# Layer 0's norm by node tile along the free axis, with the first chunk of neighbour sums in its loop, and layer 1's reciprocal denominators through memory

## The chip, the cores and the metric

The kernel runs on one core of one Trainium2 chip. The metric is the device time of one execution in microseconds; the time of a kernel is the median of its runs.

## The reference

Four graph layers stand one after the other, each on the normed and rectified input and each with a residual. The batch is 8, there are 2048 nodes with 64 features, and 64 hyperedges.

```python
h = jnp.maximum(_layernorm(x, axis=-1), 0.0)
x = x + L0(h, H, adj, ...)   # layer 0
h = jnp.maximum(_layernorm(x, axis=-1), 0.0)
x = x + L1(h, adj, W, a)     # layer 1
...                          # layers 2 and 3 in the same form
```

Layer 0 has two halves whose results are mixed by a learned softmax. One is the mean over neighbours, `einsum('nm,bmf->bnf', adj / deg, h @ W_ind)`, called `industry` below. The other goes through the hyperedges of each node. Layer 1 is a masked attention over the neighbours:

```python
e = leaky_relu(s_src[:, :, None] + s_dst[:, None, :], 0.2)
attention = softmax(where(adj > 0.5, e, -9e15), axis=2)
return elu(attention @ h)
```

Layers 2 and 3 are repeated products with the adjacency matrix, small maps of the features, and in layer 3 a map that differs from node to node.

## The kernel before

The 8 batches make 4 pairs, `NP`; a pair's 2 x 64 features fill 128 partitions. The 2048 nodes make 16 tiles of 128 (`NT`) and 4 chunks of 512 (`NCW`). A tensor named with T, or `hn[p]`, has features on the partitions and nodes along the free axis.

The program is written with a tile framework. Its scheduler puts the instructions into each engine's queue in an order of its own, and can move loads, memsets and products forward. Where an order is to hold, the code says so: `InOrder` keeps each instruction of an engine in written order, and `kit.strict` does this for matrix products and transposes. Each queue runs in its order, so an instruction that waits holds up all behind it. The SP queue issues most loads and stores, and the POOL queue (GpSimd) issues the adjacency loads and the DMAs that add into memory.

Layer 0, as far as it matters here:

- **Norm** (L882 to L912): for each pair and each half of the nodes (`HN` = 1024), `x` is loaded from `xT` with features on the partitions. `kit.norm` (L739) gets mean and variance by products with `kit.avg`, a 128x128 matrix that averages over each batch's 64 partitions, then Square, Ln and Exp on ScalarE and the rest on VectorE. The result `hn[p]` is multiplied with `W_ind` (`py`, L902) and stored as two parts `Y[0]`, `Y[1]`, high and low.
- Between the pairs come `pairs` (L833, numbers the pairs of node and hyperedge: `rank`, `Q`, `slot`, `mid`, `width`), `weights` (L813) and the weights of layers 1 and 2.
- **Industry** (L926): for each chunk of 512 nodes, eight loads `at` of two row tiles of the adjacency, and for each row tile 4 pairs x 2 parts = 8 products into the four banks `acc`. VectorE adds the adjacency rows (`ds`, L945) for the degrees. After a row tile's 8 products, one entry of the list `units` is run. `units` holds the other half's work: `members` (L963; products `ph`, `pg`, `pd`; stores to `hi_dram` and `lo_dram`), the tables and the bias rows of layer 3. At a chunk's end the sums are moved to `ev`, divided by the degree (`rdeg`) and stored.

The gather stage of layer 0 follows at about 248 us, then its output stage, and from about 495 us layer 1.

**Layer 1** (`attend`, L1543) runs for each pair and each half of the nodes, so 8 times. For each of the 16 row tiles `m`, VectorE makes two score tiles `pt` (L1572), and TensorE multiplies them into `o` (features) and `dn` (denominators, each repeated over 32 partitions). In the next half's loop, `between(m)` runs the leftovers of the last: at m = 1 `total(0)`, at m = 2 `end`. `total(k)` spreads the denominators to the 64 partitions of each batch with a product by the matrix `wide` (`prd`, L1586) and takes Ln; `end` does the second one, Exp, and `res = o * den` (L1593), the ELU and a DMA that adds into `x1_dram`.

Of the kernel before, what the change touches and what calls it, by code (L numbers as in the profile page):

```python
# [8 lines left out]
FP = mybir.dt.float32  # L9
# [625 lines left out]
class Kit:  # L635


    def __init__(self, tc, t, pool):
# [13 lines left out]
        self.wide = pool.tile([P, P], FP, name="wide")  # L652
        nc.vector.memset(self.wide, 0.0)
        for q in range(4):
            nc.vector.memset(self.wide[32 * q : 32 * q + 32, half(q % 2)], 1.0 / 32)
# [19 lines left out]
    def block_diag(self, pool, src, name):  # L675
        return self.block_diag_in(pool.tile([P, P], FP, name=name), src)
# [7 lines left out]
    def layer1_weights(self, pool, ps):  # L684

        nc, t = self.nc, self.t
        W = self.block_diag(pool, t["L1_gnn_W"], "W1f")
        WT = self.block_diag(pool, t["L1_gnn_WT"], "W1Tf")
        a4 = pool.tile([P, 4], FP, name="a4")
        nc.vector.memset(a4, 0.0)  # L690
        for b2 in range(2):
            nc.sync.dma_start(out=a4[half(b2), b2 : b2 + 1], in_=t["L1_gnn_a"][F : 2 * F, :])
            nc.sync.dma_start(out=a4[half(b2), 2 + b2 : 3 + b2], in_=t["L1_gnn_a"][0:F, :])
        nc.vector.tensor_copy(self.W1x[:, 0:P], W)
        pw = ps.tile([P, 4], FP, tag="yy", name="pw1")
        nc.tensor.matmul(pw, WT, a4, start=True, stop=True)
        nc.vector.tensor_copy(self.W1x[:, P : P + 4], pw)

    def layer2_weights(self, pool, ps):
# [5 lines left out]
        W2n = self.block_diag(pool, t["L2_gnn_W2"], "W2n")  # L705
# [4 lines left out]
        for dst, w in ((self.Wvc, self.W1v), (self.Wec, self.W1e)):  # L710
            pw = ps.tile([P, P], FP, tag="yy", name="pw2")
            mm(pw, W2n, w, start=True, stop=True)
            nc.vector.tensor_copy(dst, pw)
        pw = ps.tile([P, 1], FP, tag="yy", name="pwc")
        mm(pw, self.W1v, self.b2c, start=True, stop=True)
        nc.vector.tensor_add(self.b1c, pw, self.b1)
        r = pool.tile([P, P], FP, name="b2r")
        for h in range(2):
            nc.vector.tensor_scalar(r[:, half(h)], self.ones, self.b2c, None, op0=OP.mult)
        pw = ps.tile([P, P], FP, tag="yy", name="pwb")  # L720
# [41 lines left out]
def layer0(kit, hn, x1_dram, open_early, late_tile, between):  # L762
# [40 lines left out]
    with ExitStack() as sA:  # L803
# [9 lines left out]
        def weights(pool, ps):  # L813

            W = kit.block_diag(pool, t["L0_gnn_W"], "W0f")
            WT = kit.block_diag(pool, t["L0_gnn_WT"], "W0Tf")
# [12 lines left out]
            pw = ps.tile([P, 4], FP, tag="yy", name="pw")  # L829
# [3 lines left out]
        def pairs(pool, ps):  # L833


            tmp = pool.tile([P, SLOTS], mybir.dt.int32, name="iota_i")
            nc.gpsimd.iota(tmp, pattern=[[1, SLOTS]], base=0, channel_multiplier=0)
            nc.vector.tensor_copy(slot, tmp)
            tri = pool.tile([P, P], FP, name="tri")
            nc.gpsimd.iota(tmp[:, 0:P], pattern=[[1, P]], base=0, channel_multiplier=-1)  # L840
            nc.vector.tensor_copy(tri, tmp[:, 0:P])
            nc.vector.tensor_scalar(tri, tri, 0.0, None, op0=OP.is_ge)
            for h in range(2):
                nc.sync.dma_start(out=M[:, :, h, :], in_=t["L0_gnn_H"].rearrange("(t p) e -> p t e", p=P))
            Mf = M.rearrange("p t h e -> p (t h e)")
            nc.vector.tensor_scalar(Mf, Mf, 0.0, None, op0=OP.is_gt)
            nc.sync.dma_start(out=MT, in_=t["HT"])
            nc.vector.tensor_scalar(MT, MT, 0.0, None, op0=OP.is_gt)
            rank = pool.tile([P, NT, E], FP, name="rank")
            deg = pool.tile([P, NT], FP, name="deg")  # L850
            first = pool.tile([P, NT], FP, name="first")
            past = pool.tile([P, NT], FP, name="past")
            for g in range(2):
                pr = ps.tile([P, 8, E], FP, tag="yy", name="pr")
                for k in range(8):
                    i = 8 * g + k
                    mm(pr[:, k, :], MT[:, i * P : (i + 1) * P], tri[0:E, 0:E], start=True, stop=True)
                nc.vector.tensor_copy(rank[:, 8 * g : 8 * g + 8, :], pr)
            nc.vector.tensor_copy(deg, rank[:, :, E - 1])
            pc = ps.tile([P, NT], FP, tag="yy", name="pc")  # L860
            mm(pc, tri, deg, start=True, stop=True)
            nc.vector.tensor_copy(past, pc)
            nc.vector.tensor_sub(first, past, deg)

            nc.vector.tensor_tensor(rank, rank, first[:, :, None].to_broadcast([P, NT, E]), op=OP.add)
            nc.vector.tensor_tensor(rank, rank, M[:, :, 0, :], op=OP.mult)
            for h in range(2):
                nc.vector.tensor_scalar(Q[:, :, h, :], rank, -1.0, None, op0=OP.add)
            nc.vector.tensor_tensor(mid, first, past, op=OP.add)
            nc.vector.tensor_scalar(mid, mid, -0.5, 0.5, op0=OP.mult, op1=OP.add)  # L870
            nc.vector.tensor_scalar(width, deg, 0.5, None, op0=OP.mult)

            lo = pool.tile([P, NT], FP, name="bad_t")
            nc.vector.tensor_reduce(bad[:, 0:1], deg, AX.X, OP.min)
            nc.vector.tensor_scalar(bad[:, 0:1], bad[:, 0:1], 0.5, None, op0=OP.is_lt)
            nc.vector.tensor_scalar(lo, past, SLOTS + 0.5, None, op0=OP.is_gt)
            nc.vector.tensor_reduce(bad[:, 1:2], lo, AX.X, OP.max)
            nc.vector.tensor_reduce(bad[0:E, 2:3], MT, AX.X, OP.max)
            nc.vector.tensor_scalar(bad[0:E, 2:3], bad[0:E, 2:3], 0.5, None, op0=OP.is_lt)


        with ExitStack() as s1:  # L882
            pool = s1.enter_context(tc.tile_pool(name="rank", bufs=1, reuse_waits="tile"))
            sb = s1.enter_context(tc.tile_pool(name="nf_sb", bufs=2, reuse_waits="tile"))
            ps = s1.enter_context(tc.tile_pool(name="nf_ps", bufs=2, space=PSUM, reuse_waits="tile"))
            kit.use_ln_exp()
            for p in range(NP):
                for hf in range(2):
                    s = cols(hf, HN)
                    x = sb.tile([P, HN], FP, tag="x", name="x", bufs=3)  # L890
                    for k in range(2):
                        nc.sync.dma_start(out=x[:, cols(k)], in_=t["xT"][p, :, cols(2 * hf + k)])
                    mean = ps.tile([P, HN], FP, tag="mean", name="mean", bufs=1)
                    var = ps.tile([P, HN], FP, tag="var", name="var")
                    xc = sb.tile([P, HN], FP, tag="xc", name="xc")
                    q = sb.tile([P, HN], FP, tag="q", name="q")
                    kit.norm(hn[p][:, s], x, mean, var, xc, q)
                    for c in (2 * hf, 2 * hf + 1):
                        py = ps.tile([P, 4, P], FP, tag="yy", name="py")
                        for k in range(4):  # L900
                            m = 4 * c + k
                            mm(py[:, k, :], hn[p][:, m * P : (m + 1) * P], W_ind, start=True, stop=True)  # L902
                        yh = Y[0][:, 4 * c : 4 * c + 4, p, :]
                        nc.scalar.copy(yh, py)
                        nc.vector.tensor_tensor(Y[1][:, 4 * c : 4 * c + 4, p, :], py, yh.bitcast(FP), op=OP.subtract)
                if p == 0:
                    pairs(pool, ps)
                if p == 1:
                    weights(pool, ps)
                    kit.layer1_weights(pool, ps)  # L910
                if p == 2:
                    kit.layer2_weights(pool, ps)  # L912

        with ExitStack() as s1:
            sp = s1.enter_context(tc.tile_pool(name="streamf", bufs=6, reuse_waits="tile"))
# [10 lines left out]
            def industry(c):  # L926

                acc = [ps.tile([P, CW], FP, tag=f"acc{p}", name=f"acc{p}") for p in range(NP)]
                ds = sb.tile([P, 2, CW], FR, tag="ds", name="ds")
                for g in range(NT // 2):  # L930
                    at = sp.tile([P, 2, CW], FR, tag="at", name="at")
                    nc.gpsimd.dma_start(
                        out=at,
                        in_=t["adjT"][g * 2 * P : (g + 1) * 2 * P, cols(c)].bitcast(FR).rearrange("(k p) n -> p k n", p=P),
                    )
                    for k in range(2):
# [4 lines left out]
                        if units:  # L941
                            units.pop(0)()
# [3 lines left out]
                    was = at  # L946
                ev = [sb.tile([P, CW], FP, tag="ev", name="ev", bufs=4) for p in range(NP)]
# [147 lines left out]
            last = None  # L1095
            for i in range(NT):
                begin_, part_, end_ = members(i)
                units += [begin_, part_] + ([last] if last else [])
                last = end_
            units += [last, table_1]  # L1100
# [4 lines left out]
            for c in range(NCW):  # L1105
# [274 lines left out]
class Layer1:  # L1380
# [6 lines left out]
    def __init__(self, kit, x1_dram):  # L1387
# [5 lines left out]
        self.r_dram = dram.tile([NP, 2, N], FP, name="r_dram")  # L1393
# [702 lines left out]
```

## Time and profile before

| | us |
|---|---|
| runs: median (lowest, highest) of 3 | 2019.26 (2017.56, 2027.6) |
| profiled execution | 2014.73 |
| its span on the core | 2012.8 |
| norm of layer 0, from the start | 70 |
| neighbour sums, four chunks | 70 to 248 |
| gather stage and output stage | 248 to 495 |
| layer 1's attention | 495 to 916 |
| layers 2 and 3 | 916 to the end |

The profile is of one execution. PE is TensorE's products, PEld its weight loads, DVE is VectorE, ACT ScalarE, POOL GpSimd, SP the engine that issues DMAs. A group's line gives line, engine, operation, output<-inputs, tile shape and count, then the busy time, the mean of one in ns, and the engine's idle time just before with what ended it. A timeline's line begins with start and length. A product of float32 operands has two records. Matrix products are pipelined, so a record lasts longer than the time to the next one's start.

### The profile page before, as it was taken

What the parts mean: (1) busy time and instruction counts of PE and PEld (TensorE: products, weight loads), DVE (VectorE), ACT (ScalarE), POOL (GpSimd) and SP (SyncE); (2) the same over time, 40 slices, a digit from 0 to 9 for tenths busy, and PEclk for the clock granted to TensorE, in tenths of its full rate; (3) what the DMA queues carried; (4) which work ended last, traced back from release to release, by engine and by line L of the source; (5) the groups of instructions that cost most, each with busy time, mean ns of one, the idle gap of its engine ahead of it and who ended that gap; (6) DMA issues with size and microseconds to landing.
All of it is one profiled execution on the core that took longest, in us unless ns stands there. A gap on an engine that the chain in (4) does not pass through costs nothing.

```text
span 2012.8 us, 23432 instructions
## 1 busy us (share of the span) xinstructions
PE 1955.4 (97%) x9124; PEld 1153.8 (57%) x9124; DVE 1215.2 (60%) x1899; ACT 444.3 (22%) x827; POOL 294.8 (15%) x399
## 2 busy tenths in 40 slices
PE   7999899978999999999999999999999999999997
PEld 4777777623323223227776467775477755577654
DVE  6666499966888888883234752326632356533366
ACT  4312255566112121112130011210111200112100
POOL 0211077621000000000001210002200012101022
PEclk8999999999999999999999999999999999999999
DMA  6666264176011111114110011201022100122000
GB/s 175 199 182 190 80 225 141 43 216 129 28 43 37 48 37 32 47 28 92 55 45 22 19 43 60 58 12 31 23 63 61 32 22 20 44 62 57 11 19 13
DMA packets 84248, 138.14 MB, mean 69 GB/s; under 512 B 32752, under 2 KB 33008, under 8 KB 81456
## 3 DMA queue, kind: packets, MB, share of 16 engines
q1 hardware_dynamic: 65200, 83.86, 14.3%
q0 software_dynamic: 18928, 52.70, 10.4%
q8 instruction: 74, 1.21, 0.2%
q14 instruction: 46, 0.38, 0.1%
HBM read 102.64 MB, written 37.03 MB: 69 GB/s over the span
## 4 chain that ended last, share of the span: by engine, by line
PE 79%; issue 7%; DVE 4%; DMA 3%; ACT 3%; POOL 2%; SPq 1%; POOLq 0%; ACTq 0%; DVEq 0%
PE acc L726 27%; PE u L726 13%; PE o L726 11%; PE dn L726 6%; PE acc L940 3%; PE pd L726 3%; PE pgs L726 2%; PE py L726 2%; PE var L726 2%; PE mean L726 2%; PE pm L726 1%; DMA iv<-ind_dram 1%; DMA at<-in_adjT 1%; PE ph L726 1%; PE pv L726 1%
## 5 line engine op out<-in xcount | busy, mean ns | idle before, releaser
L726 PE MATMUL acc<-aT,parts 128*128 128x512 f32 x1664 | 448.3, 415 | 0.0
L726 PEld LDWEIGHTS acc<-aT,parts 128*128 128x128 f32 x1664 | 306.4, 188 | 102.3 <-issue 39.8
L1972 DVE TENSOR_TENSOR pr<-u,embf 128x512 f32<-128x512 f32 x256 | 170.6, 688 | 171.4 <-PE u L726 163.7
L1572 DVE SCALAR_TENSOR_TENSOR pt<-R,wd,aT 128x1024 f32<-128x1024 f32 x192 | 236.5, 1280 | 18.2 <-PE dn L726 6.6
L726 PE MATMUL u<-W3f,y 64*128 64x512 f32 x1024 | 244.3, 589 | 0.0
L726 PE MATMUL o<-pt,hS 128*64 128x512 f32 x1024 | 236.4, 599 | 0.8 <-DVE pt L1572 0.6
L726 PEld LDWEIGHTS u<-W3f,y 64*128 64x128 f32 x1024 | 102.9, 187 | 117.9 <-issue 117.9
L726 PEld LDWEIGHTS o<-pt,hS 128*64 128x64 f32 x1024 | 68.0, 136 | 159.2 <-issue 150.5
L726 PE MATMUL u<-W3f,v 64*128 64x512 f32 x512 | 138.9, 607 | 0.0
L940 PE MATMUL acc<-at,Y 128*128 128x512 f32 x512 | 134.1, 406 | 1.8 <-DVE ev L949 1.8
L726 PE MATMUL dn<-pt,vd 128*32 128x512 f32 x1024 | 123.1, 598 | 0.0
L1984 POOL TENSOR_TENSOR fold<-fold 128x256 f32<-128x256 f32 x64 | 47.8, 746 | 506.6 <-DVE fold L1983 506.6
L1789 DVE TENSOR_TENSOR yb<-py,cb_f 128x512 f32<-128x512 f32 x32 | 22.1, 691 | 165.2 <-PE py L726 165.2
L940 PEld LDWEIGHTS acc<-at,Y 128*128 128x128 f32 x512 | 93.5, 191 | 21.8 <-DVE ev L949 2.6
L726 PE MATMUL acc<-aTl,parts 128*128 128x512 f32 x384 | 96.5, 393 | 0.0
L1976 DVE TENSOR_TENSOR pr<-pr 128x512 f32<-128x512 f32 x128 | 88.3, 690 | 2.2
L1572 DVE SCALAR_TENSOR_TENSOR pt<-R,wd,aTl 128x1024 f32<-128x1024 f32 x64 | 79.8, 1282 | 11.4 <-PE dn L726 8.2
L1879 POOL TENSOR_TENSOR bq<-bq,xp 128x512 f32<-128x512 f32 x16 | 20.6, 1290 | 434.1 <-ACT xp L1862 434.1
L726 PEld LDWEIGHTS u<-W3f,v 64*128 64x128 f32 x512 | 51.8, 186 | 56.1 <-issue 34.3
L726 PEld LDWEIGHTS acc<-aTl,parts 128*128 128x128 f32 x384 | 72.1, 188 | 16.9
L726 PEld LDWEIGHTS dn<-pt,vd 128*32 128x32 f32 x1024 | 26.7, 108 | 80.8 <-issue 74.6
L630 POOL TENSOR_TENSOR mix<-ex,wt 128x512 f32<-128x512 f32 x64 | 67.8, 1061 | 34.8 <-DVE ex L630 29.0
(332 smaller groups left out, 2668.5 us busy)
## 6 DMA issues: line engine op xcount, KB each, us to landing
at<-in_adjT POOLq DMA_DIRECT2D x32, 512.0 KB, 4.7
raw<-in_adjT SPq DMA_DIRECT2D x64, 256.0 KB, 3.4
aT<-in_adjT POOLq DMA_DIRECT2D x12, 1024.0 KB, 5.3
xp<-xd SPq DMA_DIRECT2D x45, 256.0 KB, 3.4
R<-r_dram SPq DMA_DIRECT2D x14, 512.0 KB, 3.8
hi_dram<-hi SPq DMA_DIRECT2D x16, 264.0 KB, 2.4
lo_dram<-lo SPq DMA_DIRECT2D x16, 264.0 KB, 3.5
hhi<-hi_dram POOLq DMA_DIRECT2D x16, 264.0 KB, 3.1
```

What stands on the lines that cost most here:

```text
L630: self.tc.keep_in_program_order(getattr(self.engine, name)(*args, **kw))
L726: one = self.nc.tensor.matmul(*args, **kw)
L940: mm(acc[p], Y[h][:, m, p, :], at[:, k, :], start=m + h == 0, stop=m == NT - 1 and h == 1)
L1572: nc.vector.scalar_tensor_tensor(pt, R[b2], wd[:, m, b2 : b2 + 1], aT[m][:, s].bitcast(FP), op0=OP.max, op1=OP.mult)
L1789: nc.vector.tensor_tensor(yb, py, bias[:, None, :].to_broadcast([P, 4, P]), op=OP.add)
L1879: nc.gpsimd.tensor_add(bq, bq, xp)
L1972: nc.vector.tensor_tensor(a, u[h], emb[:, i, 8 * w : 8 * w + 8, None].to_broadcast([P, 8, F]), op=OP.mult)
L1976: nc.vector.tensor_add(pr[h], pr[h], a)
L1984: nc.gpsimd.tensor_add(fold[:, :, 0:2, :], fold[:, :, 0:2, :], fold[:, :, 2:4, :])
```

## The change

The norm of layer 0 is made for each tile of 128 nodes, with the nodes on the partitions, from a new input `xN` (a copy of x in the order node, batch, feature). Sums over 64 features are VectorE reduces along the free axis; GpSimd subtracts the mean, ScalarE squares, VectorE scales. Four transposes for each tile (`turns`) bring it into `hn`'s layout. The products with `W_ind`, the two parts of `Y`, and the 8 products of the first chunk's sums for this tile follow in the same loop with lags of 3, 4 and 5 tiles. The loop has 21 passes; all four engines are kept in written order. In this chunk GpSimd adds the degrees.

The numbering of the pairs becomes `listing`, seven entries for the list of units; the weights of layers 1 and 2 become two more. `weights` and two comparisons (`marks`) stand ahead of the second chunk. The remaining three chunks run two units after the first row tile of a load and one after the second.

In layer 1, ScalarE takes Ln and Exp of the denominators in place; a DMA writes one row for each batch and chunk to memory (`d_dram`), and two DMAs read them back spread over 64 partitions into `den`. `total` and the matrix `wide` go. `end` is run at m = 3.

```diff
+            def load(i):
+                xs[i] = sb.tile([P, B * F], FP, tag="x", name="x", bufs=5)
+                nc.sync.dma_start(out=xs[i], in_=t["xN"][i * P : (i + 1) * P, :])
+            def sums(i):
+                st[i] = sb.tile([P, 2, B], FP, tag="st", name="st", bufs=4)
+                V.tensor_reduce(st[i][:, 0], groups(xs[i]), AX.X, OP.add)
+                V.tensor_scalar(st[i][:, 0], st[i][:, 0], -1.0 / F, None, op0=OP.mult)
+            def centred(i):
+                xc[i] = sb.tile([P, B * F], FP, tag="xc", name="xc", bufs=4)
+                G.tensor_tensor(groups(xc[i]), groups(xs[i]), spans(st[i][:, 0]), op=OP.add)
+            def squares(i):
+                A.activation(xs[i], xc[i], AF.Square)
+            def sums2(i):
+                V.tensor_reduce(st[i][:, 1], groups(xs.pop(i)), AX.X, OP.add)
+            def scales(i):
+                A.activation(st[i][:, 1], st[i][:, 1], AF.Ln, bias=kit.eps, scale=1.0 / F)
+                A.activation(st[i][:, 1], st[i][:, 1], AF.Exp, scale=-0.5)
+            def scaled(i):
+                V.scalar_tensor_tensor(
+                    groups(xc[i]), groups(xc[i]), 0.0, spans(st.pop(i)[:, 1]), op0=OP.max, op1=OP.mult
+                )
+            def turns(i):
+                tp[i] = ps.tile([P, NP, P], FP, tag="tp", name="tpx")
+                x = xc.pop(i)
+                for p in range(NP):
+                    kit.turn(tp[i][:, p, :], x[:, p * P : (p + 1) * P])
+            def turned(i):
+                d = tp.pop(i)
+                for p in range(NP):
+                    A.activation(hn[p][:, i * P : (i + 1) * P], d[:, p, :], AF.Copy)
+            def maps(i):
+                py[i] = ps.tile([P, NP, P], FP, tag="yy", name="py")
+                for p in range(NP):
+                    kit.mm(py[i][:, p, :], hn[p][:, i * P : (i + 1) * P], W_ind, start=True, stop=True)
+            def halves(i):
+                A.activation(Y[0][:, i], py[i], AF.Copy)
+                V.tensor_tensor(Y[1][:, i], py.pop(i), Y[0][:, i].bitcast(FP), op=OP.subtract)
+            def spread(m):
+                for p in range(NP):
+                    for h in range(2):
+                        kit.mm(acc[p], Y[h][:, m, p, :], at[m // 2][:, m % 2, :], start=m + h == 0, stop=m == NT - 1 and h == 1)
+            def degrees(g):
+                if g:
+                    G.tensor_tensor(ds, (at[0] if g == 1 else ds).bitcast(FP), at[g].bitcast(FP), op=OP.add)
...
+            for i in range(4):
+                load(i)
+            for g in range(6):
+                at[g] = rows_of(0, g)
...
+            kit.strict = True
+            for j in range(NT + 5):
+                on = lambda k: 0 <= j - k < NT
+                if 0 < j and j + 3 < NT:
+                    load(j + 3)
+                for lag, step in (
+                    (0, sums), (0, centred), (1, squares), (1, sums2), (2, turns), (3, maps),
+                    (4, halves), (1, scales), (1, scaled), (2, turned), (5, spread),
+                ):
+                    if on(lag):
+                        step(j - lag)
+                m = j - 5
+                if m > 0 and m % 2:
+                    degrees(m // 2)
+                    if 1 <= m // 2 and m // 2 + 5 < NT // 2:
+                        at[m // 2 + 5] = rows_of(0, m // 2 + 5)
+            kit.strict = False
...
-                        if units:
-                            units.pop(0)()
+                        for _ in range(2 - k):
+                            if units:
+                                units.pop(0)()
...
+            weights(small, ps)
+            marks()
+            last, rest = None, listing(ps)
+            rest += [lambda: kit.layer1_weights(small, ps), lambda: kit.layer2_weights(small, ps)]
             for i in range(NT):
                 begin_, part_, end_ = members(i)
                 units += [begin_, part_] + ([last] if last else [])
+                if i % 2 and rest:
+                    units.append(rest.pop(0))
                 last = end_
+            units += rest
...
-            for c in range(NCW):
+            out_of(0, acc, ds)
+            for c in range(1, NCW):
                 industry(c)
...
         nc.vector.tensor_scalar_max(ds, dn, 1e-30)
+        nc.scalar.activation(ds, ds, AF.Ln)
+        nc.scalar.activation(ds, ds, AF.Exp, scale=-1.0)
+        rows = self.d_dram[hf]
+        nc.gpsimd.dma_start(out=rows, in_=ds.rearrange("(q r) n -> q r n", r=32)[:, 0, :])
         den = sb.tile([P, HN], FP, tag="den", name="den", bufs=1)
-        def total(k):
-            pr = ps.tile([P, CW], FP, tag="r", name="prd", bufs=1)
-            mm(pr, wide[half(k), :], ds[half(k), :], start=True, stop=True)
-            nc.scalar.activation(den[:, cols(k)], pr, AF.Ln)
+        for b2 in range(2):
+            nc.gpsimd.dma_start(
+                out=den[half(b2), :].rearrange("p (k n) -> p k n", k=2),
+                in_=rows.rearrange("(k b) n -> b k n", b=2)[b2 : b2 + 1].to_broadcast([F, 2, CW]),
+            )
         def end():
-            total(1)
-            nc.scalar.activation(den, den, AF.Exp, scale=-1.0)
             r = sb.tile([P, HN], FP, tag="res", name="res", bufs=1)
...
-        return [lambda: total(0), end]
+        return [lambda: None, lambda: None, end]
```

## The prediction

> **What bounds the kernel now.** I read the page's engine shares first, then the sliced busy rows, then the busy table over stretches that I cut at the stages, then groups and timelines inside the two stages that the change touches. From the page:
>
> ```profile
> PE 1955.4 (97%) x9124; PEld 1153.8 (57%) x9124; DVE 1215.2 (60%) x1899; ACT 444.3 (22%) x827; POOL 294.8 (15%) x399
> ...
> PE   7999899978999999999999999999999999999997
> ```
>
> TensorE is in use nearly everywhere, and the weak digits stand at the very start and near 200 and 410 to 500 us. A busy PE is modelled and need not run at full rate, so I look at stretches (columns: length; busy us and instructions of PE, weight load, DVE, ACT, POOL; granted clock; DMA share; GB/s):
>
> ```profile
> 0.00:70.00 70.00, 56.86 (x239) 35.27 (x240) 43.82 (x94) 34.81 (x40) 5.96 (x14) 0.93 0.61 172
> 70.00:247.00 177.00, 168.26 (x807) 133.28 (x805) 106.01 (x270) 36.36 (x121) 23.34 (x33) 0.98 0.54 163
> ...
> 500.00:930.00 430.00, 429.30 (x2325) 134.38 (x2325) 367.74 (x372) 74.53 (x124) 6.85 (x8) 1.00 0.16 39
> ```
>
> The first stretch is layer 0's norm. Nothing is full there: PE idles 13 us, and part of its busy time runs at half rate (below). The second is the four chunks of neighbour sums, bound by PE (95%). The third is the attention of layer 1: PE is full, DVE has 62 us to spare. So PE work taken out of the third stretch should pay nearly in full, and PE work of the second that can be laid into the holes of the first pays too.
>
> In the first stretch the norm's means and variances are products with a 128x128 averaging matrix:
>
> ```profile
> L726 PE MATMUL mean<-x,avg_f 128*128 128x512 f32 x32 | 19.3, 728 | 6.7 <-DMA x<-in_xT 4.1 <-DVE xc L745 2.5
> L726 PE MATMUL var<-q,avg_f 128*128 128x512 f32 x32 | 16.4, 637 | 1.4 <-ACT q L746 1.4
> ```
>
> and for a while the array is slow: these four mean records took 3.78 us, while other groups of four took 1.98.
>
> ```profile
> 24.25 5.96 PE L857 MATMUL pr<-tri,MT 64*128 64x64 f32 x32 [1.33 <-DVE Y L905]
> 30.13 3.78 PE L726 MATMUL mean<-x,avg_f 128*128 128x512 f32 x4
> ```
>
> Unit prices for a norm along the free axis come from the same form of norm in the last layers (groups between 1000 and 1010 us):
>
> ```profile
> L1879 POOL TENSOR_TENSOR bq<-bq,xp 128x512 f32<-128x512 f32 x1 | 1.3, 1283 | 79.8 <-ACT xp L1862 79.8
> L1868 DVE SCALAR_TENSOR_TENSOR vn<-st,xp 128x512 f32<-128x512 f32 x1 | 1.2, 1166 | 0.0
> ...
> L1873 DVE SCALAR_TENSOR_TENSOR vn<-vn,st 128x512 f32<-128x512 f32 x1 | 0.7, 691 | 0.6 <-ACT st L1872 0.6
> ...
> L1866 DVE TENSOR_REDUCE st<-xp 128x8 f32<-128x512 f32 x1 | 0.7, 686 | 2.2 <-ACT xp L1862 2.2
> ```
>
> The rate of the sums comes from the timeline, a run of 53 in 12.20 us, 0.230 us each:
>
> ```profile
> 197.57 12.20 PE L940 MATMUL acc<-at,Y 128*128 128x512 f32 x53
> ```
>
> In layer 1 the timeline shows what a denominator product costs: it sits alone between other products, and the next starts 1.05 us later.
>
> ```profile
> 555.25 1.12 PE L726 MATMUL prd<-ds,wide 64*128 64x512 f32 x2
> ...
> 556.30 1.13 PE L726 MATMUL var<-q,avg_f 128*128 128x512 f32 x2
> ```
>
> **What the Trainium skill says.** "TensorE: Matmul & The Clock Gate", Part 1: the array runs at half clock until it has been busy for a window of about 3.4 us, and falls back after an idle one. The trace agrees in kind: the first mean records took 1.22 us each, those from 9 us on 0.59. "GPSIMD Engine Reference", Specifications: POOL shares its SBUF port with DVE instructions that have two SBUF inputs. The trace agrees: L1868, beside POOL's L1879, took 1.17 us where its like L1873 took 0.69. "DMA: Bandwidth & Descriptors", Anatomy of one DMA: a transfer has a fixed 2 us, mostly the write's receipt. The trace's small loads landed in 2.1 to 2.6 us.
>
> **The change, part by part.**
>
> *Norm, PE.* Out go 64 mean and var records at 0.43 us (8 in 3.60 us in a full-rate stretch): 27.5 us. In come 64 transposes; four of the same kind stand as 0.60 us, so 0.14 each, 9 us. The 128 py records stay.
>
> *The loop's period.* One tile costs, in steady state: PE 0.6 (four turns) + 0.95 (eight py records at 0.12) + 8 x 0.230 = 1.85 (sums), 3.4 together. DVE: two reduces 0.69 each, a small scale 0.15, the STT 0.69 to 1.17, the subtraction 0.69: 2.9 to 3.4, less some overlap of neighbours. ACT: square 0.63, copy 0.585, Ln 0.30, Exp 0.21, and four 128x128 copies. The trace has those only with a bias column, 0.361 us; I take 0.30: 2.9. POOL: centring, 1.06 (mix) to 1.28 (bq); the degree adds of 128x1024 it has nowhere, so twice those, 2.1 to 2.6, every second tile; average 2.1 to 2.6. All queues are in written order. Inside a tile ACT and DVE pass the work to and fro: square 0.63, reduce 0.69, Ln and Exp 0.5, STT 0.7 to 1.2, about 0.1 for each hand-over: 3.0 to 3.5. So the period lies between 3.4 (PE alone) and the 4.6 that it would be if a third of the hand-overs were exposed; I take 3.6. There are 21 passes: 5 us until the first tile is loaded, 5 filling passes at 2.8, 16 full ones at 3.6: **the loop ends at 77 us**. Bounds: 70 and 98.
>
> *What starts beside it.* Six adjacency loads of 512 KB are issued on POOL before the first centring (0.71 each, 4.3 us; the first tile's sum is ready at about 5, so 1 us late). They, four x tiles and M and MT make 5.5 MB, some 25 us at the 200 to 230 GB/s of the early trace. That can hold tiles 4 to 6; x is three tiles ahead. 0 to 6 us, I take 2 within the filling passes. SP carries the same 16 x loads; the 35 or so small weight loads (0.6 us each, a solid block on SP from 12 to 39 us in the chain of waits, with x queued behind) now come after the loop in the text. The scheduler can pull them forward, as it now pulls their memsets to 2 to 3 us. If it doesn't, Wx is some 11 us late, covered by chunk 1's sums if those are put ahead: 0 to 8 us, I take 0.
>
> *Second stage.* It now runs from 70 to 247.7: 177.7 us. One of four chunks leaves: 128 x 0.230 = 29.4. The listing comes in with 32 small records at 0.12, 3.8, and the weight products with 3: 155. DVE loses the seven adds of chunk 0 (8.5 us) and gains marks (2.4), listing (about 12) and weights (3): 115 of 155, still second. Three units rather than two between 32 sums keep pairs of ph buffers apart by over 5 us, so I put no wait there. The tables no longer fall on the start of a chunk, where ev's buffers and eT collide (PE idles 2 us, 210 to 213); I leave that as reserve. **End at 232, minus 16.**
>
> *Denominators.* Out go 16 products (four pairs of batches, two halves, two chunks) at 1.05 us of PE: 16.8, in a stretch where PE is full. ACT does Ln and Exp on 512 columns (1.2) instead of Ln twice and Exp on 1024 (2.3). New is the way through memory: ds, 1.2 us of ACT, POOL issue 0.9, write 2.2, two reads 1.7 + 3.8 (R's rows take 3.8): 10 us. POOL has nothing else there but one add per half (0.86). Waiting is `res` on DVE, and behind it the pt's. Now ds at 549.7 and `res` at 564.3 are 14.6 us apart, and the change puts `end` one step later, so 10 us fit. DVE goes from 86% to 89%. If half of the transfers come late by 1 to 2 us, 3 pts in store cover most. The last one is not near the end: it is followed by layer 2. I take **minus 15**, between minus 17 and plus 5.
>
> Sum: 16 + 15 = 31. The profiled execution took 2014.7 (span 2012.8 and 1.9 around it): 1983.7. The median shown, 2019.3, is 4.5 higher: **1988**.
>
> **The rivals.**
> *The loop stands on its hand-overs* (18%): the period is 4.4 rather than 3.6; 21 x 0.8 = 17 us are lost, and only layer 1 pays: 2005. For it: ACT and DVE alternate inside each tile, and POOL slows DVE. Against: lags of one to five tiles.
> *The denominators come late* (8%): DVE waits 2 us in each half, and PE's saving becomes idle time: 2003. Against: the 14.6 us.
> *TensorE runs the loop at half clock* (14%, the case on the other side): per tile 2 x 3.4 = 6.8, so 16 x 3.2 = 51 us more: 2039. For it: at 24 to 34 us it did just this with gaps of 1 to 3 us around it. Against: at 6.8 it would be busy without a gap and so speed up. It decides from a mean period of 5.1, where 21 x 1.5 eats the 31; half of the loop at half clock costs 25 and leaves the time within half a percent.
> *It does not move the work* (5%): the scheduler puts weights and listing in front of the loop's end, the holes fill with waits for x, and layer 1 returns little: 2012.
> The likeliest case has 55%.
>
> **How the numbers follow.** About half a percent, 10 us, is what a measurement tells from no change. Faster by more (below 2009): 0.55 and most of the next two, 0.75. Within it, a tail of each and the last: 0.11. Slower: 0.14. Low end: loop at 70 and no stall left in the second stage (12 us) with 17 in layer 1: 1967. High end: 2020, which leaves the half-clock case out.
>
> **What would show it.** No mean or var records before 250 us; `acc` records from 20 us on; loop over near 77 and chunk 4's last sums near 228; `acc` at 0.23 in the loop; no `prd`; `res` not waiting for a DMA over 1 us. Wrong if loop ends past 95, if sums in it take 0.46, or if PE in 500 to 915 shows idle time.

## The result, and the profile after

The median is 2013.43 us over 7 runs (2011.53 to 2021.7), against 2017.83 us for the kernel before (7 runs beside it). The ratio is 0.9981, with a 95% interval of 0.9957 to 1.0006, so no gain is shown. The prediction was 1988, or 0.985. The profiled execution took 2020.19 us (span 2018.3), 6.8 above its own median; the one before took 2014.73, 3.1 below its median. So the two profiles lie 5.5 us apart in the other direction than the medians, and a difference of that size between them means little by itself.

The page's engine shares and the PE row of its 40 slices, of the kernel after:

```profile
PE 1926.3 (95%) x9092; PEld 1148.0 (57%) x9092; DVE 1232.7 (61%) x1940; ACT 437.2 (22%) x907; POOL 343.2 (17%) x446
...
PE   3899999987999999999999999999999999999997
```

PE lost 29 us of busy time, as the change intends, and yet the time is nearly the same: its first digit is now 3, where it was 7. The busy table over stretches cut at the new stages (length; busy us and instructions of PE, weight load, DVE, ACT, POOL; granted clock; DMA share; GB/s):

```profile
0.00:28.50 28.50, 0.00 (x0) 0.00 (x0) 8.58 (x22) 1.91 (x2) 7.91 (x16) 1.00 0.89 216
28.50:96.00 67.50, 56.93 (x324) 48.40 (x325) 60.83 (x98) 35.98 (x129) 36.30 (x28) 0.97 0.49 148
96.00:257.00 161.00, 150.77 (x714) 119.09 (x714) 94.63 (x281) 33.45 (x116) 16.84 (x25) 0.93 0.51 154
257.00:513.00 256.00, 232.15 (x997) 140.39 (x996) 208.24 (x315) 142.38 (x272) 128.75 (x137) 0.94 0.55 147
513.00:930.00 417.00, 413.93 (x2284) 128.03 (x2285) 368.59 (x372) 66.03 (x116) 22.06 (x32) 1.00 0.20 49
```

For 28.5 us PE has no instruction at all. DVE works 8.6 us in them, and the DMA engines are busy for 89%. Then the rest of the loop takes 67 us. What PE waits for up to 96 us is one line in the table of waits (us in total, times, longest):

```profile
PE tpx L729 <- DVE xc L630: 39.1, 8, 30.7
```

The 30.7 us are the time before the first transpose. What DVE does meanwhile is in its timeline (start, length, then in brackets the idle time ahead and what ended it):

```profile
5.05 1.08 DVE L630 TENSOR_SCALAR st<-st 128x8 f32<-128x8 f32 x1
22.53 1.23 DVE L1174 TENSOR_SCALAR M<-M 128x2048 f32<-128x2048 f32 x1 [16.40 <-DMA M<-in_L_gnn_H]
25.11 1.22 DVE L1175 TENSOR_SCALAR MT<-MT 64x2048 f32<-64x2048 f32 x1 [1.35 <-DMA MT<-in_HT]
26.37 2.28 DVE L883 TENSOR_REDUCE bad<-MT 64x1 f32<-64x2048 f32 x1
28.57 0.67 DVE L630 TENSOR_REDUCE st<-x 128x8 f32<-128x512 f32 x1
```

The loop's own instructions are those of L630. After the sums of two tiles stand three instructions that belong behind the loop: the two comparisons of `marks` and a reduce of `widths`. The scheduler put them there, and they wait for M and MT. DVE's queue is held from 6.1 to 28.6. M is late because SP, which issues it, is slow, and because the data then come late: its second load landed at 22.4, 17.7 us after its issue began (8.8 before). SP's timeline of the same execution:

```profile
4.02 8.88 SPq L973 DMA_DIRECT2D M<-in_L_gnn_H  x2
12.94 5.00 SPq L974 DMA_DIRECT2D MT<-in_HT  x1
17.99 0.58 SPq L912 DMA_DIRECT2D x<-in_xN  x1
18.70 1.11 SPq L678 DMA_DIRECT2D W0f<-in_L_gnn_W  x2
```

In the kernel before, the same issues took 3.48 and 2.12 us:

```profile
4.31 3.48 SPq L844 DMA_DIRECT2D M<-in_L_gnn_H  x2
7.84 2.12 SPq L847 DMA_DIRECT2D MT<-in_HT  x1
```

The Trainium skill, "Perfetto Trace Analysis", section DMA Instruction — HWDGE (DVE, Sync), says what this length is: the record ends after all descriptors are generated, and there may be more of them than the buffer holds. The trace agrees in that the two issues of M grew by 5.4 us together with six adjacency loads of 512 KB under way beside them; e5 and e7 below test that. What SP spends the added time on, no run shows.

Once it runs, the loop's sums start 3.18 us apart at first. From 57 to 76 us they start 3.18 and 4.46 us apart in turn, 7.64 for two tiles:

```profile
56.57 2.09 PE L723 MATMUL acc<-at,Y 128*128 128x512 f32 x8
...
61.02 2.09 PE L723 MATMUL acc<-at,Y 128*128 128x512 f32 x8
...
64.20 2.10 PE L723 MATMUL acc<-at,Y 128*128 128x512 f32 x8
```

The slower of the two is the step in which POOL adds the degrees. POOL's timeline of the first such step, then DVE's:

```profile
49.08 2.40 POOL L630 TENSOR_TENSOR ds<-at 128x1024 fp32r<-128x1024 f32 x1
```

```profile
46.35 0.69 DVE L630 SCALAR_TENSOR_TENSOR xc<-xc,st 128x512 f32<-128x512 f32 x1
...
49.11 2.91 DVE L630 SCALAR_TENSOR_TENSOR xc<-xc,st 128x512 f32<-128x512 f32 x1
```

DVE's scaling of 0.69 us takes 2.91 beside the add; it ends 0.54 us after it. The skill's "GPSIMD Engine Reference", Specifications, says that POOL shares its SBUF interfaces with VectorE, with contention when a DVE instruction has two inputs in SBUF. This trace agrees.

Layer 1 went as planned. From its first `o` to layer 2's first `acc` it took 420.9 us before (495.60 to 916.45) and 407.1 after (512.88 to 919.94): minus 13.8. DVE waited for the way through memory five times (the table of waits, 513 to 945 us), longest, 2.8 us, in the last half, where layer 2 follows:

```profile
DVE res L1686 <- DMA den<-d_dram: 7.3, 5, 2.8
```

PE stood idle for only 3.1 of the 417 us from 513 to 930 (the last line of the busy table).

### The profile page after: what moved, and what is told of

Read it like the earlier page. It is cut to its first block, busy times and chain, and to the rows that moved or that the text cites. A ratio compares the mean times of both kernels' runs of the same rounds, so it can differ in the third digit from the quotient of the medians.

```text
span 2018.3 us, 23591 instructions
## 1 busy us (share of the span) xinstructions
PE 1926.3 (95%) x9092; PEld 1148.0 (57%) x9092; DVE 1232.7 (61%) x1940; ACT 437.2 (22%) x907; POOL 343.2 (17%) x446
## 3 DMA queue, kind: packets, MB, share of 16 engines
q0 software_dynamic: 20464, 56.96, 11.3%
## 4 chain that ended last, share of the span: by engine, by line
PE 59%; issue 20%; DVE 8%; DMA 7%; ACT 3%; POOL 2%; SPq 1%; POOLq 0%; DVEq 0%; ACTq 0%
PE acc L723 23%; PE u L723 13%; PE o L723 3%; PE pd L723 3%; PE pgs L723 2%; PE acc L1013 2%; PE py L723 2%; DMA den<-d_dram 2%; DMA at<-in_adjT 2%; PE dn L723 1%; PE pm L723 1%; DVE xc L630 1%; PE mean L723 1%; PE var L723 1%; DVE pt L1663 1%
## 5 line engine op out<-in xcount | busy, mean ns | idle before, releaser
L1663 DVE SCALAR_TENSOR_TENSOR pt<-R,wd,aT 128x1024 f32<-128x1024 f32 x192 | 235.9, 1277 | 9.5 <-DMA R<-r_dram 2.7
L1013 PE MATMUL acc<-at,Y 128*128 128x512 f32 x384 | 109.1, 425 | 1.1 <-DVE ev L1026 1.1
L1013 PEld LDWEIGHTS acc<-at,Y 128*128 128x128 f32 x384 | 71.6, 196 | 18.2 <-issue 3.5
L630 POOL TENSOR_TENSOR mix<-ex,wt 128x512 f32<-128x512 f32 x64 | 67.8, 1061 | 34.6 <-DVE ex L630 27.6
```

The costliest lines, as they stand in the source:

```text
L630: self.tc.keep_in_program_order(getattr(self.engine, name)(*args, **kw))
L1013: mm(acc[p], Y[h][:, m, p, :], at[:, k, :], start=m + h == 0, stop=m == NT - 1 and h == 1)
L1663: nc.vector.scalar_tensor_tensor(pt, R[b2], wd[:, m, b2 : b2 + 1], aT[m][:, s].bitcast(FP), op0=OP.max, op1=OP.mult)
```

## The experiments

All ratios are to the kernel before, measured beside them on the same chip; its medians there were 2017.8 (the kernel after), 2016.0 (e1 to e4), 2016.3 (e5 to e8) and 2015.2 (e9, e10). The ratios are not quite the quotients of these medians. Medians are of all runs of a kernel, the times to the right of the ratio are us of the profiled execution.

| | median | ratio (95%) | loop's last sums end | gather's first `px` | layer 1's first `o` |
|---|---|---|---|---|---|
| before | | 1 | (norm: 70) | 245.6 | 495.6 |
| after | 2013.4 | 0.9981 (0.9957 to 1.0006) | 95.5 | 260.0 | 512.9 |
| e1_den_alone | 2000.7 | 0.9933 (0.9902 to 0.9964) | (norm) | 244.7 | 494.0 |
| e2_norm_alone | 2027.4 | 1.0047 (1.0032 to 1.0062) | 96.1 | 252.7 | 510.2 |
| e3_marks_late | 2011.2 | 0.9975 (0.9962 to 0.9989) | 93.8 | 254.1 | 511.0 |
| e4_deg_dve | 2007.2 | 0.9953 (0.9940 to 0.9966) | 88.2 | 248.4 | 502.0 |
| e5_sp_late | 2007.8 | 0.9953 (0.9938 to 0.9968) | 86.0 | 241.1 | 502.0 |
| e6_sp_late_deg | 2002.8 | 0.9927 (0.9900 to 0.9954) | 80.4 | 235.9 | 496.2 |
| e7_few_at | 2004.3 | 0.9942 (0.9927 to 0.9958) | 85.9 | 242.2 | 496.2 |
| e8_dve_free | 2009.7 | 0.9958 (0.9943 to 0.9973) | 88.8 | 244.6 | 503.2 |
| e9_all | 1993.8 | 0.9884 (0.9865 to 0.9904) | 73.5 | 231.8 | 487.8 |
| e10_few_deg | 1999.5 | 0.9922 (0.9905 to 0.9939) | 79.4 | 234.5 | 492.6 |

**The two halves of the change, each alone.** e1 is the kernel before with layer 1's denominators through memory; e2 is the kernel after with the denominators as they were.

```diff
-            total(1)
-            nc.scalar.activation(den, den, AF.Exp, scale=-1.0)
+        nc.scalar.activation(ds, ds, AF.Ln)
+        nc.scalar.activation(ds, ds, AF.Exp, scale=-1.0)
+        rows = self.d_dram[hf]
+        nc.gpsimd.dma_start(out=rows, in_=ds.rearrange("(q r) n -> q r n", r=32)[:, 0, :])
...
```

> The kernel before with the second part of the change alone: reciprocal denominators of layer 1 through memory. Theory (layer 1 gained what was forecast, and the norm part gave it back): about 14 us faster than before, ratio near 0.993, layer 1 from its first o product to the last prd or py some 14 us shorter, no prd. Rival (the way through memory made DVE wait and layer 1 gave nothing): ratio 1.000 and DVE or PE idle time at res in layer 1.

> The changed kernel with layer 1's denominators put back as before: the norm part alone. Theory: some 9 us slower than before, ratio near 1.004, the loop ending at about 96 us and the sums at about 257 us as in the changed kernel's trace. Rival (the norm part is neutral or a gain, and layer 1 lost): ratio 0.993 to 1.000.

Both came as expected. Layer 1's half gains 0.67% (13.5 us by the ratio, 15.4 by the medians) and the norm's half loses 0.47% (9.5 us by the ratio, 11.4 by the medians). The question is the second half, on which 16 us of gain were forecast.

**What holds the loop at its start.** e3 keeps the two comparisons in written order, so that they come after the loop.

```diff
             def marks():
+                V = InOrder(tc, nc.vector)
-                nc.vector.tensor_scalar(Mf, Mf, 0.0, None, op0=OP.is_gt)
+                V.tensor_scalar(Mf, Mf, 0.0, None, op0=OP.is_gt)
...
```

> The changed kernel with the two comparisons of marks kept in written order on DVE, so after the loop. Theory (they were pulled ahead of the loop's steps on DVE and held them until M and MT had landed, 22 us): the wait for M goes; tile 4, whose load stands behind M and MT on SP until 18 us, is late next and lands at about 22 us, so some 14 of the 22 us come back: ratio to before near 0.991, loop end near 82 us. Rival (the loads fill the first 25 us whatever DVE does, or PE and the hand-overs set the loop): the loop end stays near 96 us and the ratio near 0.998.

It missed. The loop ended 1.7 us sooner, not 13, and the numbers are the rival's. Another instruction that the scheduler had put in the same place took over the wait. DVE's timeline of e3:

```profile
26.39 0.23 DVE L825 COPY W0x<-W0f 128x128 f32<-128x128 f32 x1 [20.26 <-DMA W0f<-in_L_gnn_W]
```

W0f is issued on SP at 19.55, behind M and MT. So the comparisons were one waiter of several, and all of them waited for loads that SP issued late. Four kernels take this apart. e5 issues M and MT in the loop, keeps x in order, and has no later instruction with a wait ahead of the loop on DVE. e8 does only the last of these. e7 leaves everything and issues four of the six early adjacency loads later. e6 is e5 with e4's edit.

In e5, e6 and e9:

```diff
+                if j in (8, 10):
+                    S.dma_start(out=M[:, :, j // 2 - 4, :], in_=t["L0_gnn_H"].rearrange("(t p) e -> p t e", p=P))
+                if j == 12:
+                    S.dma_start(out=MT, in_=t["HT"])
```

In e5, e6, e8 and e9, with e3's edit; the pool is opened ahead of `e_sb`, so that it lies in memory that the loop frees:

```diff
+            small = s1.enter_context(tc.tile_pool(name="small_w", bufs=1, reuse_waits="tile"))
             sb = s1.enter_context(tc.tile_pool(name="e_sb", bufs=2, reuse_waits="tile"))
...
-            nc.vector.tensor_scalar(Av, ones, av, None, op0=OP.mult)
+            nc.vector.tensor_scalar(Av, ones_r[:, 0:F].bitcast(FP), av, None, op0=OP.mult)
```

In e7, e9 and e10:

```diff
-            for g in range(6):
+            for g in range(2):
                 at[g] = rows_of(0, g)
...
+                if j in (3, 5, 7, 8):
+                    g = {3: 2, 5: 3, 7: 4, 8: 5}[j]
+                    at[g] = rows_of(0, g, G)
```

> The loads of M and MT are issued on SP in the loop's steps 8, 10 and 12, the x loads keep their order among them, and nothing of the later code stands on DVE ahead of the loop's steps with a wait for a load (marks after the loop, the weights of layer 0 in memory that the loop frees, Av from ones_r). Theory (the loop starts 22 us late because DVE waits for loads that SP issues late): DVE goes on at about 6 us, the same 67 us of loop follow, its last sums are near 75 us and the second stage's near 236, 20 us under the changed kernel: ratio 0.988. Rival (the loop is bound by its own transfers, 8 MB of x and adjacency, and only starts late because nothing could go on): the loop's last sums stay past 88, ratio 0.995 or more.

> As the first of these, but M and MT are loaded where the changed kernel loads them, ahead of the loop. Theory (the hold of DVE by waits of later code is the whole of the late start; SP's 14 us for M and MT alone would be hidden by the four x tiles issued before them): loop's last sums near 77 us, ratio 0.989. Rival (SP is the cause by itself: x tile 5 is issued at 18 us and the small weight loads stand ahead of the next x tiles): the steps from tile 4 on wait for x, last sums at 84 to 88, ratio 0.993.

> The changed kernel with two adjacency loads ahead of the loop instead of six; the four others are issued in its steps 3, 5, 7 and 8. M and MT stay where they are on SP. Theory A (SP needs long to issue M and MT because the DMA rings are full of adjacency): M's two issues take under 5 us together instead of 8.9, MT's under 3 instead of 5.0, x tile 5 is issued by 12 us, the compare of M starts before 17, the loop's last sums come near 85, ratio 0.993. Theory B (it is M's and MT's own short runs): the issues stay at 8 and 5 us, the loop's last sums stay past 91, ratio 0.997.

Neither e8 nor e5 is what the theory said: e8 came out just past the rival's loop end and past its time; e5 had its loop end between its two answers and the rival's ratio. With no later instruction ahead of the loop's steps on DVE (e8), DVE runs four tiles and then stands before the fifth x tile, which SP issued at 18.33:

```profile
26.70 0.69 DVE L630 TENSOR_REDUCE st<-x 128x8 f32<-128x512 f32 x1 [11.08 <-DMA x<-in_xN]
```

With M and MT out of the way as well (e5), the place on SP is taken by some twenty other loads, most of them of small weights, and the sixth x tile is issued at 21.26. SP's timeline of e5, and below it DVE's:

```profile
19.94 1.22 SPq L1335 DMA_DIRECT2D xd<-in_xT  x2
21.26 0.53 SPq L630 DMA_DIRECT2D x<-in_xN  x1
...
37.39 0.43 SPq L630 DMA_DIRECT2D M<-in_L_gnn_H  x1
```

```profile
29.03 0.69 DVE L630 TENSOR_REDUCE st<-x 128x8 f32<-128x512 f32 x1 [10.64 <-DMA x<-in_xN]
```

Both tiles took about 8 us from issue to landing (18.33 to 26.7, 21.26 to 29.0), so the traffic delays them twice, at the issue and after it. M takes 0.43 us to issue here, in mid-loop. In e7 M has its old place. SP's and DVE's timelines of e7:

```profile
4.02 6.66 SPq L973 DMA_DIRECT2D M<-in_L_gnn_H  x2
10.72 1.97 SPq L974 DMA_DIRECT2D MT<-in_HT  x1
```

```profile
16.04 1.23 DVE L1177 TENSOR_SCALAR M<-M 128x2048 f32<-128x2048 f32 x1 [8.49 <-DMA M<-in_L_gnn_H]
```

MT's issue fell from 5.00 to 1.97 as theory A says, M's from 8.88 only to 6.66 (under 5 was expected); x went out at 12.73, and the loop ended at 85.9, both about as A says. But the two loads of M are not alike. The view of M by tile gives the shorter issue, the mean and the longer one in ns, here of the kernel before, the kernel after, e7 and e5:

```profile
L844 SPq DMA_DIRECT2D M<-in_L_gnn_H x2: 434/1722/3009, 4.3 to 4.8; - x2
```

```profile
L973 SPq DMA_DIRECT2D M<-in_L_gnn_H x2: 662/4420/8178, 4.0 to 4.7; - x2
```

```profile
L973 SPq DMA_DIRECT2D M<-in_L_gnn_H x2: 882/3310/5738, 4.0 to 4.9; - x2
```

```profile
L630 SPq DMA_DIRECT2D M<-in_L_gnn_H x2: 426/427/428, 37.4 to 45.1; - x2
```

The first load of M is issued in under 1 us everywhere. Before, after and in e7 it is the second, right behind it, that takes long, and it takes longer with more adjacency under way. In e5 the two stand 8 us apart, with less traffic: the x load behind the first took 0.33 us, and the first had landed (at 43.4) before the second was issued. So an issue gets long by what is in flight; how much of that is M's own first load and how much the loads of others is not separated.

**The price of the degree adds on POOL.** e4 makes them on DVE.

```diff
-                    G.tensor_tensor(ds, (at[0] if g == 1 else ds).bitcast(FP), at[g].bitcast(FP), op=OP.add)
+                    V.tensor_tensor(ds, (at[0] if g == 1 else ds).bitcast(FP), at[g].bitcast(FP), op=OP.add)
```

> The changed kernel with the degree adds of the first chunk on DVE rather than POOL. Theory (a POOL add of 2.4 us keeps DVE's two-input STT from running beside it: 2.82 us rather than 0.69 in every second tile): STT stays near 0.7 us, DVE gains seven adds of 1.22; 15 us of waits go and 8.5 us come: 5 to 7 us less in the loop, ratio to before near 0.995. Rival (the long STT is a matter of dependencies, not of the port): STT still near 2.8 us in every second tile, and the loop 8 us longer.

As expected. The groups of this line between 28 and 95 us (count, busy us, mean ns), first of the kernel after, then of e4:

```profile
L630 DVE SCALAR_TENSOR_TENSOR xc<-xc,st 128x512 f32<-128x512 f32 x16 | 22.9, 1432 | 1.7 <-ACT st L630 0.7
...
L630 POOL TENSOR_TENSOR ds<-ds,at 128x1024 fp32r<-128x1024 f32 x6 | 14.6, 2431 | 0.1
```

```profile
L630 DVE SCALAR_TENSOR_TENSOR xc<-xc,st 128x512 f32<-128x512 f32 x16 | 11.2, 700 | 1.7 <-ACT st L630 0.7
...
L630 DVE TENSOR_TENSOR ds<-ds,at 128x1024 fp32r<-128x1024 f32 x6 | 7.3, 1218 | 0.0
```

The scaling falls back to 0.70 us, and the add itself takes half as long on DVE. DVE gets 8.5 us of adds, loses 11.7 us in the scaling, and the loop ends 7.3 us sooner.

**Both causes together, and a version that beats both kernels.** e6 joins e5 with the degree adds on DVE, and e10 joins e7 with them. e9 joins all three, and gives x eight buffers instead of five, so that eight x tiles are issued before the small loads.

```diff
-                xs[i] = sb.tile([P, B * F], FP, tag="x", name="x", bufs=5)
+                xs[i] = sb.tile([P, B * F], FP, tag="x", name="x", bufs=8)
...
-            for i in range(4):
+            for i in range(7):
                 load(i)
```

> As the one before, and the degree adds of the loop on DVE instead of POOL. Theory (the two causes add: late start 20 us, port blocking 8 us of the loop, of which the run with the adds on DVE alone kept 6): loop's last sums near 68 us, ratio 0.985. Rival (the loop with an early start is bound by DVE, which now has 1.1 us more in every second step, or by its transfers): no better than the one before, 0.988.

> The changed kernel with two edits only: two adjacency loads ahead of the loop instead of six, and the degree adds on DVE. Theory (the late start and the port blocking are separate and add): 3.9 thousandths and 2.8 thousandths off the ratio of the changed kernel, 0.9914; loop's last sums near 78 us instead of 95 (85.7 with the first edit alone, 8 less with the second). Rival (both edits relieve the same limit): 0.994, last sums no earlier than 84.

> e6_sp_late_deg (M and MT in the loop, no later instruction on DVE with a wait ahead of the loop, degree adds on DVE), with x in eight buffers instead of five, so that eight x tiles are issued on SP before the small weight loads, and with two adjacency loads ahead of the loop instead of six. Theory (what kept the loop from 70 us in e5 and e6 was SP again: the sixth x tile stood behind some twenty small loads and DVE waited 11 us for it): no wait for x over 2 us, 20 steps of about 3.1 us from 6 us on, last sums near 72 instead of 81.5, ratio 0.988. Rival (the loop is then held by adjacency that comes too late, or by the transfers of x): PE or DVE wait as long for at or x as before, last sums past 80, ratio 0.993.

e6 misses its forecast (0.9927, not 0.985) by what e5 had missed already: the sixth x tile is late again, by 11.3 us. Its loop ends 5.6 us before e5's, so the degree adds still count, nearly as much as in e4. e10 came as expected: two edits in the kernel after take it from 0.9981 to 0.9922. e9 also came as expected in loop end and ratio, and is the fastest: 0.9884 (0.9865 to 0.9904), its interval clear of 1 and of the interval of the kernel after. The busy table of e9, the loop and the second stage:

```profile
6.00:73.50 67.50, 57.74 (x323) 50.08 (x323) 55.60 (x104) 35.66 (x129) 23.49 (x28) 0.95 0.80 224
73.50:229.00 155.50, 147.64 (x717) 116.59 (x717) 98.60 (x289) 34.06 (x117) 17.48 (x25) 0.95 0.52 160
```

In mid-loop its sums start 3.18 us apart, step after step, with PE not waiting: 20.50, 23.68, 26.86, up to 52.33. That is the PE-bound period. Then the scheduler's hand shows once more: a degree add of the second chunk stands between the loop's steps on DVE and waits for its load, PE stands idle for 3.3 us, and SP was held for 13.65 us by an x tile behind the first load of M. DVE's and SP's timelines of e9:

```profile
54.43 1.23 DVE L1025 TENSOR_TENSOR ds<-at 128x1024 fp32r<-128x1024 f32 x1 [2.59 <-DMA at<-in_adjT]
```

```profile
26.93 0.39 SPq L630 DMA_DIRECT2D M<-in_L_gnn_H  x1
29.49 13.65 SPq L630 DMA_DIRECT2D x<-in_xN  x1
```

## Why the prediction was wrong

**The start of the loop: this step failed.** The sum had 5 us until the first tile, 2 us for what else is in flight, and for the small weight loads on SP "0 to 8 us, I take 0". The stall was 22.4 us (6.1 to 28.6). Each number that it needed was in view: M and MT on SP ahead of further x tiles, 5.5 MB at the rate of the early trace, and a scheduler that moves things forward. The 25 us for the traffic were right: MT landed at 25.1 us and the x of tile 4 at 25.7. What was wrong is the 2 us of delay drawn from them: the stall was priced as late tiles that a lead of three tiles hides. Three things were not priced: that an issue on SP grows while loads are in flight (M and MT, 5.6 us before, 13.9 after), that x of tile 4 stands behind it, and that DVE, whose order is kept within the loop only, gets foreign instructions with waits of their own put ahead. "All four engines are kept in written order" holds for the loop's own instructions alone. e3, e8 and e5 take a part of these away and gain 2, 7 and 10 us at the loop's end. e7 thins out the traffic and gains 10. In e9 the first sums start at 20.50 us instead of 40.13: 19.6 of the 22.4 us are back. Its loop ends 22.0 us sooner, 73.5 against 95.5, but that has the degree adds on DVE in it too.

**The loop's pace: the size was right by errors that cancel.** The forecast from the second pass on was about 69 us; it took 67 in the kernel after. The period was not 3.6: from 40.13 to 87.05 us twelve steps took 3.91 on the mean. They are 3.18 in undisturbed tiles, 4.46 in three of those with a degree add, and 6.83 in one before which DVE also made an add of the second chunk that the scheduler had moved in (at 75.47). On the other side the last three tiles' sums ran in one go, in 5.73 us, where the sum had three periods:

```profile
89.79 5.73 PE L723 MATMUL acc<-at,Y 128*128 128x512 f32 x24
```

The prediction had the port in the price of the scaling, 0.69 to 1.17; it measured 2.91. Its example was read as a slower instruction. The timelines of the kernel before show a wait:

```profile
1003.92 1.28 POOL L1879 TENSOR_TENSOR bq<-bq,xp 128x512 f32<-128x512 f32 x1 [79.82 <-ACT xp L1862]
```

```profile
1004.59 1.17 DVE L1868 SCALAR_TENSOR_TENSOR vn<-st,xp 128x512 f32<-128x512 f32 x1
```

There too DVE ended 0.56 us after POOL, whose instruction was half as long as the degree add. PE alone was put at 3.4 and is 3.18.

**The second stage: the work was right, the clock was not in it.** From the loop's end to the gather's first `px` 153 us were forecast (155 to 247.7 in the view of before, which is 2.1 behind `px`). Nine kernels with the new norm took 155.1 to 160.3, the profiled execution after 164.5. e2 has the same code there and took 156.6. The granted clock, the share of TensorE's full clock that the profile reports as given, accounts for the difference. Length times (1 - clock), added up over short windows, is what was lost to it: 12.6 us in the kernel after, 5.1 in e2, 1.8 to 10.3 in the others. Length less loss is 149.4 to 153.3 in all ten, 151.9 after and 151.5 in e2. The busy table of the stage, first of the kernel after, then of e2 (the third number from the end is the clock):

```profile
95.50:260.00 164.50, 152.13 (x719) 119.69 (x717) 97.10 (x287) 35.09 (x118) 18.41 (x26) 0.92 0.50 151
```

```profile
96.10:252.70 156.60, 146.10 (x719) 114.60 (x717) 97.28 (x287) 34.96 (x118) 18.42 (x26) 0.97 0.52 158
```

The forecast was drawn from a stage that lost 3.4 us to the clock, so it stands for about 149.6 us without the loss: right within 4 us.

**The gather and output stages: left out of the sum.** Nothing in them is changed, and they took longer in every kernel with the new norm: from the first `px` to layer 1's first `o` 252.9 to 260.9 us in ten kernels, 250.0 and 249.4 in the two with the old one. The granted clock accounts for most of it. I cut the stretch into 26 windows and added up length times (1 - clock): 10.3 us lost before and 10.4 in e1, 13.1 after, 15.0 to 20.5 in the others. Length less loss is 238.0 to 243.3 everywhere (239.8 before, 239.7 after). Some 10 us at half clock from 247 us on became some 24 us from 248.5 on in the kernel after, where they begin in the second stage: its first `px` is at 260.0. The lines for it, from the busy table in steps of 10 us, first before, then after:

```profile
250.00:260.00 10.00, 9.27 (x36) 7.43 (x37) 6.08 (x10) 4.05 (x8) 3.65 (x3) 0.62 0.45 159
260.00:270.00 10.00, 10.00 (x48) 7.35 (x46) 9.36 (x15) 4.44 (x11) 9.26 (x11) 1.00 0.66 213
```

```profile
250.00:260.00 10.00, 7.86 (x25) 6.12 (x24) 4.86 (x9) 2.38 (x4) 1.56 (x1) 0.50 0.07 27
260.00:270.00 10.00, 8.23 (x26) 6.55 (x27) 7.59 (x9) 2.82 (x6) 1.56 (x1) 0.50 0.31 106
```

Over whole runs the median clock is 0.988 to 0.989 before and in e1, and 0.9825 to 0.987 in the others. Why the new norm's kernels are granted less was not tried and stays open. It is one reason why e9, whose loop ended 3.5 us sooner than forecast, stays at minus 21 us and not minus 31: the stretch cost it 6 us, the second stage 5, layers 2 and 3 1.5, and layer 1 gave 14.5 rather than 15.

**The denominators: right.** Minus 15 was forecast; it was minus 13.8 in the kernel after, and 13.5 in e1 by the ratio. `res` waits longer than the 1 us allowed, but DVE has the time.

For the kernel after in its profile: loop 18.5 us late, second stage 11.5, gather and output 2.9, layer 1 1.2, layers 2 and 3 2.0 (1096.4 to 1098.4). That is 36.1 of the 36.5 between 1983.7 and 2020.2. Some 9 us of it are this execution's clock: by the same sum over the whole span it lost 31.6 us, the profile before 22.6.

**The rivals.** The nearest was the one held least likely, 5%, "does not move the work", at 2012: the scheduler does put later work ahead. But the mechanism was not its own: the work moved, layer 1 paid, and most of the time was lost to one wait at the start. Half clock came in the loop only in passing (eight `py` records took 1.92 us at 34.20 and at 81.57, and about 1.06 else); 24 sums take 5.73 us in the kernel after, 0.24 each. The hand-overs are not exposed either, or e9 would not run at 3.18. The mark "wrong if loop ends past 95" was met, by half a microsecond. One reading of the prediction is off and changes nothing in it: 1.22 us is the mean record at 30.13; the first ones took 1.19 and 1.06.

## What to carry to other kernels

A queue kept in order is only as free as what the scheduler may put between its steps: before you price a pipelined loop, list for each of its engines what else can be moved ahead of it, and what load each of these waits for. Price the issue of a load by what is in flight when it is issued, and ask which tile stands behind it on the same queue; taking one waiter away showed only the next while the late load stayed (e3). Here a POOL add of two tiles (2.40 us) cost DVE nearly its whole length (2.2 us) when a DVE instruction with two inputs met it, and in a loop where DVE lay on the path it was cheaper on DVE. Ask of a neighbour's slow instruction whether it ran slowly or waited: a wait grows with what it waits for.

## What was not expected of the hardware

- The first of two loads of M (512 KB each) took SP 0.4 to 1.0 us to issue; the issue right behind it took 3.0 us before, 5.7 in e7, 8.2 in the kernel after, and 13.65 in e9, where it was that of an x tile. In e5, with less traffic, it took 0.33, and the second load of M, with the first landed, 0.43.
- A DVE scaling of 128x512 with two inputs took 2.91 us beside a POOL add of 2.40, against 0.69 alone: it waited for nearly all of it. The same add of 128x1024 took 2.43 us on POOL and 1.22 on DVE.
- ScalarE's copies of 128x128 out of PSUM took 0.275 us each, less than the 0.30 assumed.
